# A four-head graph attention layer aggregated with its operands swapped: pairs of heads in column groups of TensorE

## The chip, the cores and the metric

The kernel runs on one core of one Trainium2 chip. The metric is device time in microseconds of one execution. Engines are named as in the profile: PE is TensorE's matmul side, PEld its weight loads, DVE VectorE, ACT ScalarE, POOL GpSimd, SP SyncE. A matmul holds one operand in the array (the weights, up to 128 columns) and streams the other past it (the moving operand, up to 512 columns); the result lands in PSUM with one partition for each weight column.

## The reference

Four graph attention layers with pre-layernorm and residuals work on x of shape (32, 512, 256) in float32, with one 512 x 512 adjacency. The change concerns the third one, with four heads of 64 features:

```python
Wh = (h @ W).reshape(h.shape[0], h.shape[1], N_H, D_F)
s_src = jnp.einsum('bnhd,hd->bnh', Wh, a_src)
s_dst = jnp.einsum('bnhd,hd->bnh', Wh, a_dst)
e = s_src[:, :, None, :] + s_dst[:, None, :, :]
e = jnp.where(e > 0, e, NEG_SLOPE * e)
e = jnp.where(mask, e, -jnp.inf)
alpha = jax.nn.softmax(e, axis=2)
h_out = jnp.einsum('bijh,bjhd->bihd', alpha, Wh)
...
x = x + jax.nn.elu(h_out)
```

The other three layers have one head of 256 features (the last one a small network with two attentions inside). Their kernels share the helpers shown below.

## The kernel before

A batch is 512 nodes by 256 features: `NT` = 4 tiles of 128 nodes, `KF` = 2 tiles of 128 features, `NH` = 4 heads of `D` = 64 features, `CH` = 67 columns for a head.

The softmax is factored. With a query's factor taken out, the weight of key j for query i is the larger of a row value of i and a column value of j, times the mask; a key's own factor is folded into its features. So a head's weights are four DVE instructions (`weights`, line 353), one for each tile j of 128 keys: 128 keys on partitions, 512 queries along the free dimension. The row values must stand on all partitions. For head 0 that is done by four transposes on PE into a bank of PSUM. For heads 1 to 3 it goes through memory: `rows_out` (line 362) transposes the 16 columns of values, copies them to `row`, writes them to memory, and `spread` (line 372) reads each head's row back onto 128 partitions, into one of two buffers. Both transfers are issued by SP, in order.

Aggregation of a head (lines 491 to 499): for each tile t of 128 queries, four matmuls over the key tiles j hold a 128 x 128 block of the head's weights in the array and stream 65 columns of `v`: 64 features and, as the 65th, the key's factor, whose sum is the denominator. All four t's lie in one PSUM bank. DVE then takes the reciprocal of the four denominators (`reciprocal`, line 385) and multiplies the features by it, out of PSUM into `ya`. After each second head, ACT makes exp and relu of the pair's 128 features for all nodes and DVE adds the ELU to x (`add_elu`).

The order of all work is written by a planner at build time. `NS` = 4 streams each take every fourth batch. A stream is a generator; what it emits between two `yield`s stands in the engines' queues as one block. It yields the planned time of its next block, and the main loop always takes the stream with the smallest one. `after_us(n)` is the planned time of the block's start plus `STRETCH` = 2 times the TensorE cycles that the block has counted (`spent`, at 2400 cycles a microsecond) plus `SLOW` = 1.5 times n. The helper `matmul` (line 64) counts four cycles for each moving column and at least 128 columns, `transpose` (line 68) counts 256 cycles. Each stream has two banks of PSUM (`bank`) and borrows those of streams that have not begun or have ended. The weights of all streams share four buffers (tag `w`).

In layer 2 a stream makes head 0's weights and the 4.5 us of `after_us(3)` later head 1's, and from then on a head's weights are begun one head ahead of their aggregation: `begin(h + 1)`, then a wait for the planned time of head h (4.8 us after its begin at the least), then 16 matmuls.

Of the kernel before, what the change touches and what calls it, by code (L numbers as in the profile page):

```python
# [19 lines left out]
FP = mybir.dt.float32  # L20
# [3 lines left out]
AF = mybir.ActivationFunctionType  # L24
OP = mybir.AluOpType
AX = mybir.AxisListType

EPS = 1.0e-5
P = 128
# [6 lines left out]
def fast(ctx, tc, flag, x, adj, w0, a0, w1, a1, w2, a2, mlp1_w, mlp1_b, mlp2_w, mlp2_b,  # L36
         w_fc, a_fc, w_hand, a_hand, out):
    nc = tc.nc
    B, N, F = x.shape
    NT = N // P  # L40
# [3 lines left out]
    NH = a2.shape[0]  # L44
    D = F // NH
# [6 lines left out]
    work = ctx.enter_context(tc.tile_pool(name="work", bufs=2))  # L52
# [5 lines left out]
    spent = [0.0]  # L58

    def after_us(us):  # L60

        return begun[0] + STRETCH * spent[0] / CYCLES + SLOW * us

    def matmul(p, w, x, **flags):
        spent[0] += 4 * max(x.shape[-1], P)
        nc.tensor.matmul(p, w, x, **flags)  # L66

    def transpose(p, x, i, tied=False):
        spent[0] += 2 * P
        instruction = nc.tensor.transpose(p, x, i)  # L70
        if tied:
            tc.keep_in_program_order(instruction)
# [4 lines left out]
    def bank():  # L77

        own = [turn[0], *(i for i in range(NS) if i not in active and i != turn[0])]
        banks[0] += 1  # L80
        return psum.tile([P, N], FP, tag=f"b{own[banks[0] % len(own)]}", name="b", bufs=8 // NS)
# [3 lines left out]
    ident = const.tile([P, P], FP, name="ident")  # L85
# [78 lines left out]
    for h in range(NH):  # L164
        t, r = divmod(h * D, P)
# [91 lines left out]
    def small(shape, name):  # L257
        return work.tile([P] + shape, FP, tag=name, name=name, bufs=2 * NS)

    def new_xn():  # L260
        return work.tile([P, NT, F], FP, tag="xn", name="xn", bufs=3)

    def norm(xt, xn, rs, t0, late):


        st = small([2, 6], "st")
        mv = small([2, 2], "mv")
        for i in range(2):
            nc.vector.bn_stats(st[:, i, :], xt[:, t0 + i, :])  # L269
            nc.vector.bn_aggr(mv[:, i, :], st[:, i, :])  # L270
        rp = rs[:, t0:t0 + 2]
        nc.scalar.activation(rp, mv[:, :, 1], AF.Ln, bias=eps)
        nc.scalar.activation(rp, rp, AF.Exp, scale=-0.5)
        for i in range(2):
            if late:
                nc.vector.tensor_scalar(
                    xn[:, t0 + i, :], xt[:, t0 + i, :], mv[:, i, 0:1], None, op0=OP.subtract
                )
            else:
                nc.vector.tensor_scalar(  # L280
                    xn[:, t0 + i, :], xt[:, t0 + i, :], mv[:, i, 0:1], rp[:, i:i + 1], op0=OP.subtract, op1=OP.mult
                )
# [9 lines left out]
    def turned(xn, when):  # L292

        hT = work.tile([P, KF, N], FP, tag="hT", name="hT", bufs=3)
        turn_pair(xn, hT, 0)
        yield when
        turn_pair(xn, hT, 2)
        yield after_us(0.6)
        return hT
# [3 lines left out]
    def note(e):  # L303

        c = next(noted)
        nc.vector.tensor_reduce(seen[:, c:c + 1], e, AX.XY, OP.max)
# [36 lines left out]
    def weights(r_col, t_col, masked=True, r=None):  # L343

        landed = r is not None
        if not landed:
            r = bank()
            for t in range(NT):
                transpose(r[:, t * P:(t + 1) * P], r_col(t).to_broadcast([P, P]), ident)
        wt = work.tile([P, NT, N], FP, tag="w", name="w", bufs=4)  # L350
        for j in range(NT):
            if masked:
                w = nc.vector.scalar_tensor_tensor(  # L353
                    wt[:, j, :], r, t_col(j), maskT[:, j, :], op0=OP.max, op1=OP.mult
                )
                if landed and j == 0:
                    tc.keep_in_program_order(w)
            else:
                nc.vector.tensor_scalar(wt[:, j, :], r, t_col(j), None, op0=OP.max)
        return wt  # L360

    def rows_out(cols, n):

        p = bank()
        transpose(p[:NT * n, :P], cols, ident)
        row = work.tile([P, P], FP, tag="row", name="row", bufs=1)[:NT * n, :]
        nc.scalar.copy(row, p[:NT * n, :P])
        row_d = dram.tile([n, N], FP, tag="row", name="row", bufs=4)
        nc.sync.dma_start(row_d.rearrange("n (t p) -> t n p", p=P), row)
        return row_d  # L370

    def spread(row):

        r = work.tile([P, N], FP, tag="spread", name="spread", bufs=2)
        nc.sync.dma_start(r, row.partition_broadcast(P))
        return r

    def pair(tag="y"):
        return work.tile([P, 2, F], FP, tag=tag, name=tag, bufs=3)

    def aggregate(p, wt, t, rhs):
        for j in range(NT):
            matmul(p, wt[:, j, t * P:(t + 1) * P], rhs(j), start=(j == 0), stop=(j == NT - 1))

    def reciprocal(den):
        r = small([1], "rden") if len(den.shape) == 2 else small([NH, 1], "rden4")
        nc.vector.reciprocal(r, den)  # L387
        return r

# [7 lines left out]
    def averages(v, wt, t):  # L397
        p = bank()
        aggregate(p[:, :F + 1], wt, t, lambda j: v[:, j, :F + 1])
        return p[:, :F], reciprocal(p[:, F:F + 1])  # L400


    def add_elu(xr, r, q):

        nc.vector.scalar_tensor_tensor(r, q, 1.0, r, op0=OP.min, op1=OP.add)  # L405
        nc.vector.scalar_tensor_tensor(xr, r, -1.0, xr, op0=OP.add, op1=OP.add)  # L406
# [45 lines left out]
    def layer2(xt, xn, rs, when):  # L452
        hT = yield from turned(xn, when)
        v = work.tile([P, NT, NH, CH], FP, tag="v", name="v2", bufs=4)
        for t in range(NT):
            ps = bank()
            for k in range(KF):
                matmul(
                    ps[:, :NH * CH], hT[:, k, t * P:(t + 1) * P], W2[:, k, :, :], start=(k == 0), stop=(k == KF - 1)
                )  # L460
            pv = ps[:, :NH * CH].rearrange("p (h c) -> p h c", c=CH)
            nc.scalar.activation(v[:, t, :, D:], pv[:, :, D:], AF.Exp, scale=rs[:, t:t + 1])
            nc.vector.scalar_tensor_tensor(  # L463
                v[:, t, :, :D], pv[:, :, :D], rs[:, t:t + 1], v[:, t, :, D:D + 1].to_broadcast([P, NH, D]),
                op0=OP.mult, op1=OP.mult,
            )
            yield after_us(0 if t + 1 < NT else 1)
        ya = work.tile([P, NT, F], FP, tag="y4", name="y4", bufs=1)
        wts = []

        def begin(h):
            wts.append(
                weights(
                    lambda t: v[:, t, h, D + 2:D + 3], lambda j: v[:, j, h, D + 1:D + 2], r=far[h]
                )
            )
            return after_us(3.2)

        row_d = rows_out(v[:, :, :, D + 2], NH)
        far = [spread(row_d[h, :]) if h else None for h in range(NH)]
        when = begin(0)
        note(v.rearrange("p t h c -> p (t h) c")[:, :, D:])
        yield after_us(3)
        for h in range(NH):
            last = when
            if h + 1 < NH:
                when = begin(h + 1)
            yield last  # L490
            wt = wts[h]
            p = bank()
            for t in range(NT):
                aggregate(p[:, t * (D + 1):(t + 1) * (D + 1)], wt, t, lambda j: v[:, j, h, :D + 1])
            pv = p[:, :NT * (D + 1)].rearrange("p (t c) -> p t c", c=D + 1)
            r = reciprocal(pv[:, :, D:])
            nc.vector.tensor_tensor(
                ya[:, :, h * D:(h + 1) * D], pv[:, :, :D], r.to_broadcast([P, NT, D]), op=OP.mult
            )
            if h % 2:  # L500
                c = slice((h - 1) * D, (h + 1) * D)
                y = ya[:, :, c]
                q = pair("q").rearrange("p a (b f) -> p (a b) f", f=2 * D)
                nc.scalar.activation(q, y, AF.Exp)  # L504
                nc.scalar.activation(y, y, AF.Relu)  # L505
                add_elu(xt[:, :, c], y, q)
            yield after_us(0)
        xn, rs = new_xn(), small([NT], "rs")
        for t0 in range(0, NT, 2):
            norm(xt, xn, rs, t0, False)  # L510
        yield after_us(7)
        return xn, rs, after_us(2)
# [257 lines left out]
    while ready:  # L770
        i = min(ready, key=ready.get)
# [23 lines left out]
    p = bank()  # L795
# [437 lines left out]
```

## Time and profile before

| what | value |
|---|---|
| median of 3 runs | 2935.77 us |
| lowest and highest run | 2931.55, 2940.25 us |
| span of the profiled execution, first to last instruction | 2929.6 us |
| instructions | 43083 |
| DMA moved in the span | 270.89 MB, mean 92 GB/s |
| mean granted TensorE clock | 0.996 |

The profiled execution's own time is known only as its span. It lies 6.2 us below the median of the runs.

In a group of instructions, a row gives line, engine, operation, output and inputs by the program's names, shape and count, then busy time in us and mean length of one in ns, then the engine's idle time just before them and what ended most of it. A shape such as 128\*128 128x65 is a matmul with 128 rows by 128 columns of weights and 65 moving columns. Line 66 and line 70 are the helpers `matmul` and `transpose`. In a timeline a row is start, length, engine, line, operation and count of a run of alike instructions.

### The profile page before, as it was taken

Reading aid. Unit: us, or ns where it says so; the run is one execution under the profiler, and the core shown is the slowest. Engines: PE = TensorE matmul, PEld = TensorE weight load, DVE = VectorE, ACT = ScalarE, POOL = GpSimd, SP = SyncE. Lnnn points to the kernel's source line nnn. Section 1 sums busy time; section 2 is a strip of 40 time slices with the busy share of each in tenths; the row PEclk is TensorE's granted clock in tenths of the full one; section 3 lists DMA queues with packets and bytes.
Section 4 is the critical chain, followed back from the end, with each engine's and each line's share of the span. In section 5 each row is a group of like instructions: output and inputs, shape, how many; then the busy total and the mean of one; then the engine's idle time right before and its main releaser. Section 6 shows DMA issues by size and latency. Waiting matters only on the chain.

```text
span 2929.6 us, 43083 instructions
## 1 busy us (share of the span) xinstructions
PE 2858.9 (98%) x15177; PEld 2329.5 (80%) x15177; DVE 2219.9 (76%) x5676; ACT 1536.8 (52%) x3922; POOL 502.3 (17%) x515
## 2 busy tenths in 40 slices
PE   8999999999999999999999999999999999999998
PEld 6777887877888877888877888788887788877876
DVE  4677877778778778778778777787787787777764
ACT  4444455555555555555554556545555555555444
POOL 0011112112122111122021121111221111211220
PEclk9999999999999999999999999999999999999999
DMA  3033223233223333233332233222332322323230
GB/s 94 19 102 102 80 88 116 91 98 95 88 94 106 93 100 98 84 102 96 100 102 80 89 115 93 91 97 91 94 116 80 102 93 88 104 93 96 90 107 30
DMA packets 193182, 270.89 MB, mean 92 GB/s; under 512 B 17024, under 2 KB 156094, under 8 KB 192960
## 3 DMA queue, kind: packets, MB, share of 16 engines
q1 hardware_dynamic: 163200, 169.76, 18.5%
q0 software_dynamic: 29760, 98.30, 10.4%
q8 instruction: 123, 2.02, 0.3%
q14 instruction: 99, 0.81, 0.1%
HBM read 152.62 MB, written 115.39 MB: 91 GB/s over the span
## 4 chain that ended last, share of the span: by engine, by line
PE 82%; DVE 10%; ACT 4%; DMA 3%; issue 1%; SPq 0%; POOL 0%; DVEq 0%; POOLq 0%; ACTq 0%
PE b L66 75%; PE b L70 7%; DVE st L269 2%; DMA g<-table,at 2%; DVE sums L641 1%; DVE xn L280 1%; DVE x L406 1%; DVE y L405 1%; ACT v L325 1%; DVE sums L632 1%; ACT y L505 1%; ACT q L504 1%; DVE w L353 1%; ACT hT L290 1%; DVE tot L646 0%
## 5 line engine op out<-in xcount | busy, mean ns | idle before, releaser
L66 PE MATMUL b<-v,w 128*128 128x65 f32 (+1 forms) x7232 | 1218.0, 321 | 10.6 <-DVE w L353 10.5
L66 PEld LDWEIGHTS b<-v,w 128*128 128x128 f32 x7232 | 1050.0, 191 | 168.7 <-issue 56.1
L66 PE MATMUL b<-WFC,oT 128*128 128x256 f32 (+1 forms) x2048 | 495.2, 380 | 0.0
L66 PEld LDWEIGHTS b<-WFC,oT 128*128 128x128 f32 x2048 | 374.5, 189 | 49.3
L66 PE MATMUL b<-W,hT 128*128 128x259 f32 (+1 forms) x1536 | 388.8, 391 | 22.8 <-DVE v L463 14.1
L353 DVE SCALAR_TENSOR_TENSOR w<-b,v,maskT 128x512 f32<-128x512 f32 x512 | 369.4, 744 | 5.1 <-PE b L70 4.1
L607 POOL DMA_INDIRECT order<-v,at x248 | 277.0, 1117 | 490.7 <-DVE oT L730 152.3
L66 PEld LDWEIGHTS b<-W,hT 128*128 128x128 f32 x1536 | 285.3, 192 | 75.3 <-DVE v L463 17.1
L715 POOL TENSOR_TENSOR x<-x,y 128x512 f32<-128x512 f32 x62 | 87.8, 1416 | 1063.7 <-ACT y L713 950.0
L353 DVE SCALAR_TENSOR_TENSOR w<-spread,v,maskT 128x512 f32<-128x512 f32 x384 | 269.5, 742 | 0.0
L66 PE MATMUL b<-hT,WM 128*128 128x512 f32 x512 | 250.0, 599 | 0.7 <-ACT hT L290 0.7
L66 PE MATMUL b<-oT,WM 128*128 128x512 f32 x512 | 231.2, 594 | 0.0
L655 POOL DMA_INDIRECT g<-table,at x124 | 120.9, 975 | 642.8 <-ACT y L675 292.0
L387 DVE RECIPROCAL rden<-b 128x1 f32<-128x1 f32 (+1 forms) x516 | 77.3, 162 | 184.8 <-PE b L66 183.0
L529 ACT ACTIVATE v<-b,ends 128x256 f32<-128x256 f32 x256 | 118.8, 467 | 177.2 <-PE b L66 172.9
L269 DVE BATCH_NORM_STATS2 st<-x 128x6 f32<-128x256 f32 x512 | 193.3, 409 | 6.4 <-DMA x<-in_x_dram 4.1
L412 DVE TENSOR_TENSOR y<-q,y 128x512 f32<-128x512 f32 (+1 forms) x194 | 132.9, 685 | 82.9 <-ACT q L411 45.0
L339 ACT ACTIVATE oT<-b,bias 128x512 f32<-128x512 f32 x128 | 87.7, 686 | 182.7 <-PE b L66 182.0
L290 ACT ACTIVATE hT<-b 128x512 f32<-128x512 f32 x256 | 146.5, 592 | 70.3 <-PE b L70 70.2
L66 PEld LDWEIGHTS b<-oT,WM 128*128 128x128 f32 x512 | 97.5, 191 | 95.7 <-issue 92.4
L70 PE MATMUL b<-ident,xn 128*128 128x128 f32 x1024 | 147.4, 275 | 6.7 <-DVE xn L280 4.0
L70 PEld LDWEIGHTS b<-ident,xn 128*128 128x128 f32 x1024 | 123.7, 143 | 31.9 <-DVE xn L280 5.2
(143 smaller groups left out, 3748.1 us busy)
## 6 DMA issues: line engine op xcount, KB each, us to landing
table<-sums SPq DMA_DIRECT2D x62, 1032.0 KB
sums<-order SPq DMA_DIRECT2D x62, 516.0 KB
spread<-row SPq DMA_DIRECT2D x96, 256.0 KB
x<-in_x_dram SPq DMA_DIRECT2D x32, 512.0 KB
out_dram<-x SPq DMA_DIRECT2D x62, 256.0 KB
sums<-order SPq DMA_DIRECT2D x62, 129.0 KB
order<-v,at POOLq DMA_INDIRECT x248
g<-table,at POOLq DMA_INDIRECT x124
```

Of the source, the lines that this page charges most:

```text
L66: nc.tensor.matmul(p, w, x, **flags)
L70: instruction = nc.tensor.transpose(p, x, i)
L269: nc.vector.bn_stats(st[:, i, :], xt[:, t0 + i, :])
L290: nc.scalar.activation(hT[:, :, t0 * P:(t0 + 2) * P], p.rearrange("p (k n) -> p k n", k=KF), AF.Relu)
L339: nc.scalar.activation(o[:, f, :], p, AF.Relu, bias=bias[:, f:f + 1])
L353: w = nc.vector.scalar_tensor_tensor(wt[:, j, :], r, t_col(j), maskT[:, j, :], op0=OP.max, op1=OP.mult)
L387: nc.vector.reciprocal(r, den)
L412: nc.vector.tensor_tensor(r, q, r, op=OP.add)
L529: nc.scalar.activation(halves[c][:, t, :F], ps[:, :F], AF.Copy, scale=ends[:, t, 0:1])
L607: nc.gpsimd.indirect_dma_start(out=orders[c], out_offset=bass.IndirectOffsetOnAxis(ap=at[:, 0, t:t + 1], axis=0), in_=halves[c][:, t, :], ...
L655: nc.gpsimd.indirect_dma_start(out=g, out_offset=None, in_=table, in_offset=bass.IndirectOffsetOnAxis(ap=at[:, 1, t:t + 1], axis=0),)
L715: (nc.gpsimd if n == 2 else nc.vector).tensor_tensor(xr, xr, y, op=OP.add)
```

## The change

The operands of layer 2's aggregation trade places, and heads are taken in pairs. The features of a head become the weights in the array, 64 columns of them, and the 512 queries of a key tile's softmax weights are the moving operand. The two heads of a pair are put into the two halves of the array's columns by `tile_position`, in a loop over key tiles with the heads inside. The denominators have matmuls of their own: the key's factor is repeated over 32 weight columns, and four groups of 32 columns take two heads by two halves of the key tiles. Results stand transposed (features, or sums, on partitions; queries along the free dimension). ACT copies both from PSUM to SBUF (`staged`), four transposes each bring them back (`turned_back`), DVE adds the two halves of the sums, takes reciprocals for both heads at once and multiplies. The exp, relu and residual of a pair are as before.

The blocks move too. Head 1's weights are begun in the block after head 0's with `after_us(0)`, the heads of the second pair both after the first pair's matmuls, and a pair is aggregated at the earliest 9 us (`after_us(6)`) after the second of its heads is begun. The transposes back stand in a block of their own, after the next pair's begins.

```diff
@@ -64,6 +64,10 @@
     def matmul(p, w, x, **flags):
         spent[0] += 4 * max(x.shape[-1], P)
         nc.tensor.matmul(p, w, x, **flags)
+
+    def beside(p, w, x, c, **flags):
+        spent[0] += 4 * x.shape[-1] * w.shape[-1] // P
+        nc.tensor.matmul(p, w, x, tile_position=(0, c), **flags)
 
     def transpose(p, x, i, tied=False):
         spent[0] += 2 * P
@@ -383,7 +387,7 @@
             matmul(p, wt[:, j, t * P:(t + 1) * P], rhs(j), start=(j == 0), stop=(j == NT - 1))
 
     def reciprocal(den):
-        r = small([1], "rden") if len(den.shape) == 2 else small([NH, 1], "rden4")
+        r = small([1], "rden")
         nc.vector.reciprocal(r, den)
         return r
 
@@ -465,7 +469,6 @@
                 op0=OP.mult, op1=OP.mult,
             )
             yield after_us(0 if t + 1 < NT else 1)
-        ya = work.tile([P, NT, F], FP, tag="y4", name="y4", bufs=1)
         wts = []
 
         def begin(h):
@@ -474,36 +477,68 @@
                     lambda t: v[:, t, h, D + 2:D + 3], lambda j: v[:, j, h, D + 1:D + 2], r=far[h]
                 )
             )
-            return after_us(3.2)
-
-
+
+        def staged(p):
+            s = work.tile([P, N], FP, tag="y4", name="y4", bufs=2)
+            nc.scalar.copy(s, p)
+            return s
+
+        def turned_back(s):
+            p = bank()
+            for t in range(NT):
+                transpose(p[:, t * P:(t + 1) * P], s[:, t * P:(t + 1) * P], ident)
+            return p
 
         row_d = rows_out(v[:, :, :, D + 2], NH)
         far = [spread(row_d[h, :]) if h else None for h in range(NH)]
-        when = begin(0)
+        begin(0)
         note(v.rearrange("p t h c -> p (t h) c")[:, :, D:])
-        yield after_us(3)
-        for h in range(NH):
-            last = when
-            if h + 1 < NH:
-                when = begin(h + 1)
-            yield last
-            wt = wts[h]
-            p = bank()
-            for t in range(NT):
-                aggregate(p[:, t * (D + 1):(t + 1) * (D + 1)], wt, t, lambda j: v[:, j, h, :D + 1])
-            pv = p[:, :NT * (D + 1)].rearrange("p (t c) -> p t c", c=D + 1)
-            r = reciprocal(pv[:, :, D:])
+        yield after_us(0)
+        begin(1)
+        when = after_us(6)
+        half = NT // 2
+        for g in range(0, NH, 2):
+            yield when
+            fp, sp = bank(), bank()
+            for j in range(half):
+                for i in range(4):
+                    e = i // 2, i % 2 * half + j
+                    beside(
+                        sp[i * 32:(i + 1) * 32, :], v[:, e[1], g + e[0], D:D + 1].to_broadcast([P, 32]),
+                        wts[g + e[0]][:, e[1], :], i * 32, start=(j == 0), stop=(j == half - 1),
+                    )
+            s = staged(sp)
+            for j in range(NT):
+                for i in range(2):
+                    beside(
+                        fp[i * D:(i + 1) * D, :], v[:, j, g + i, :D], wts[g + i][:, j, :], i * D,
+                        start=(j == 0), stop=(j == NT - 1),
+                    )
+            f = staged(fp)
+            yield after_us(1.5)
+            if g + 2 < NH:
+                begin(g + 2)
+                yield after_us(0)
+                begin(g + 3)
+                when = after_us(6)
+                yield after_us(1.5)
+            p = turned_back(s)
+            r = small([2 * NT], "rden8")
+            nc.vector.tensor_reduce(
+                r, p.rearrange("p (e s k) -> p e s k", s=2, k=32)[:, :, :, 0], AX.X, OP.add
+            )
+            nc.vector.reciprocal(r, r)
+            p = turned_back(f)
+            y, q = pair(), pair("q")
+            y = y.rearrange("p a (b f) -> p (a b) f", f=2 * D)
+            q = q.rearrange("p a (b f) -> p (a b) f", f=2 * D)
             nc.vector.tensor_tensor(
-                ya[:, :, h * D:(h + 1) * D], pv[:, :, :D], r.to_broadcast([P, NT, D]), op=OP.mult
-            )
-            if h % 2:
-                c = slice((h - 1) * D, (h + 1) * D)
-                y = ya[:, :, c]
-                q = pair("q").rearrange("p a (b f) -> p (a b) f", f=2 * D)
-                nc.scalar.activation(q, y, AF.Exp)
-                nc.scalar.activation(y, y, AF.Relu)
-                add_elu(xt[:, :, c], y, q)
+                y.rearrange("p t (h d) -> p (t h) d", d=D), p.rearrange("p (e d) -> p e d", d=D),
+                r.unsqueeze(2).to_broadcast([P, 2 * NT, D]), op=OP.mult,
+            )
+            nc.scalar.activation(q, y, AF.Exp)
+            nc.scalar.activation(y, y, AF.Relu)
+            add_elu(xt[:, :, g * D:(g + 2) * D], y, q)
             yield after_us(0)
         xn, rs = new_xn(), small([NT], "rs")
         for t0 in range(0, NT, 2):
```

## The prediction

> **What bounds the kernel now.** I read four views, in this order: the page's busy times and its chain, the groups with shapes kept apart, the matmul part of the timeline around one head of layer 2, and the vector and queue parts of the same stretch.
>
> ```profile
> PE 2858.9 (98%) x15177; PEld 2329.5 (80%) x15177; DVE 2219.9 (76%) x5676; ACT 1536.8 (52%) x3922; POOL 502.3 (17%) x515
> PEclk9999999999999999999999999999999999999999
> PE 82%; DVE 10%; ACT 4%; DMA 3%; issue 1%; SPq 0%; POOL 0%; DVEq 0%; POOLq 0%; ACTq 0%
> ```
>
> TensorE is busy for 98% of the span at the full granted clock (0.996 by the clock view), and it carries 82% of the chain that ended last. The other engines have room: DVE idles for 24%, about 22 us in each of the 32 batches (a batch is 2929.6 / 32 = 91.6 us). So a microsecond of matmul added or removed is first taken as a microsecond of span, and work of DVE or ACT counts only where TensorE has to wait for it.
>
> ```profile
> L66 PE MATMUL b<-v,w 128*128 128x65 f32 x4096 | 476.2, 273 | 1.0 <-DVE w L353 1.0
> L66 PE MATMUL b<-hT,WM 128*128 128x512 f32 x512 | 250.0, 599 | 0.7 <-ACT hT L290 0.7
> L70 PEld LDWEIGHTS b<-ident,v 128*16 128x16 f32 x32 | 3.0, 93 | 0.5
> L387 DVE RECIPROCAL rden<-b 128x4 f32<-128x4 f32 x128 | 22.7, 177 | 83.5 <-PE b L66 83.4
> L497 DVE TENSOR_TENSOR y<-b,rden 128x256 f32<-128x256 f32 x128 | 53.3, 416 | 1.1
> L353 DVE SCALAR_TENSOR_TENSOR w<-spread,v,maskT 128x512 f32<-128x512 f32 x384 | 269.5, 742 | 0.0
> L581 ACT COPY tj<-b 128x512 f32<-128x512 f32 x31 | 17.8, 576 | 1.7 <-PE b L70 1.7
> ```
>
> The first row is the work that the change replaces. The kernel asks for 32 batches x 4 heads x 16 = 2048 of these matmuls, and the row counts 4096: a float32 matmul is two passes, one right after the other, each with its own weight load. The means (273, 599 ns) are lengths of pipelined records that overlap; the cost of a pass is the distance from one start to the next, which the timeline gives (start, length, engine, line, operation):
>
> ```profile
> 1514.76 1.88 PE L66 MATMUL b<-hT,WM 128*128 128x512 f32 x4
> 1516.48 3.63 PE L66 MATMUL b<-v,w 128*128 128x257 f32 x16
> ...
> 1544.38 0.60 PE L70 MATMUL b<-ident,y 128*128 128x128 f32 x4
> 1544.81 0.71 PE L70 MATMUL b<-ident,v 128*16 128x128 f32 x5
> ...
> 1551.00 3.68 PE L66 MATMUL b<-v,w 128*128 128x65 f32 x32
> 1554.52 0.61 PE L70 MATMUL b<-ident,y 128*128 128x128 f32 x4
> ```
>
> A pass over 512 columns costs (1516.48 - 1514.76) / 4 = 0.43 us, a transpose of 128 columns, one pass, 0.43 / 4 = 0.108 us, and a pass over 65 columns (1554.52 - 1551.00) / 32 = 0.110 us. By its columns the last should cost 0.43 x 65 / 512 = 0.055; it costs as much as 128, because each pass loads 128 columns of weights first. That waste is what the change is aimed at.
>
> **The change part by part, for one pair of heads (64 pairs in all).**
>
> Removed: 2 heads x 32 passes x 0.110 = 7.04 us of TensorE.
>
> Added, sums: 8 matmuls of 32 weight columns over 512 moving columns, 16 passes of 0.43. Added, features: 8 matmuls of 64 weight columns over 512, another 16 passes. One after another they would take 32 x 0.43 = 13.76 us; the whole change rests on several running at once in different column groups. The trace of before has no instruction that uses part of the columns beside another, so I bound it. Upper end: one pass at a time, 13.76 us. Lower end: four at a time in the sums (4 x 0.43) and two in the features (8 x 0.43), 5.16 us. What I take lies between, and comes from the order of the passes. The loop issues group 0, then 1, 2, 3, but each matmul is two adjacent passes on the same group, and in this trace passes start strictly in the order of issue, each no earlier than the columns of its predecessor on those array columns are through. If that stays so, the second pass of group 0 waits 0.43 us for the first, and the first pass of group 1 stands behind it. Then second pass and next first pass run together, never more: two in flight, whether the groups are two or four. Sixteen passes then end after 9 x 0.43 = 3.87 us, for the sums and for the features alike: 7.74 us.
>
> Added, turning back: 8 transposes x 0.108 = 0.86 us, so 8.60 us in all. Going from full array to 32-column groups, to 64-column groups and back is three switches a pair. No row shows one; below, zero (the 128*16 transpose stands among full ones at the usual spacing, 0.55 us for five); above, a full run-out of the pipe, 0.272 - 0.108 = 0.16 us each, 0.49 a pair. I take the middle, 0.25. Sum: 8.85 - 7.04 = +1.81 us a pair, x 64 = +116 us.
>
> The Trainium skill ("TensorEngine Tiling (Array Packing)", Key Properties) says that tiles run in parallel but that a change of tiling mode drains the engine, which speaks against three switches for 7 us of work; no run here shows one yet. Its page "TensorE: Matmul & The Clock Gate" (Part 3) gives 2.38 times for three column groups and says that matmuls stay in program order; by an estimate from that efficiency, 6.9 / 3.2 + 6.9 / 1.6 + 0.9 = 7.4 us, some 20 us slower over the kernel, if the two passes did not stand in each other's way.
>
> Other engines. DVE loses two reciprocals (0.177) and two multiplications (0.416), 1.19 us, and gains one small reduction (nearest row, a reduction of 12 elements, 0.156), one reciprocal (0.177) and one 512-wide multiplication out of PSUM (nearest row 0.68): 1.01. ACT gains two copies of 0.576, 74 us over the kernel, 52% to 55% busy. I cost both at nothing: the sums' copy runs beside the features' matmuls, the features' copy beside other streams, since a planned 2.25 us beyond the pair's own matmuls lie before the transposes that need it. Uncovered, the second copy would cost 64 x 0.58 = 37 us; behind it on ACT stand other streams' evacuations, for which TensorE has two banks a stream.
>
> A wait that the change adds: the weights of head 1 now follow those of head 0 at once; the planned 3 x 1.5 = 4.5 us between them are gone. They read a row that travels out to memory and back.
>
> ```profile
> 1546.19 0.68 SPq L369 DMA_DIRECT2D row<-row  x1
> 1549.54 0.82 SPq L375 DMA_DIRECT2D spread<-row  x2
> ```
> ```profile
> 1546.25 2.72 DVE L353 SCALAR_TENSOR_TENSOR w<-b,v,maskT 128x512 f32<-128x512 f32 x4
> ...
> 1555.89 1.41 DVE L353 SCALAR_TENSOR_TENSOR w<-spread,v,maskT 128x512 f32<-128x512 f32 x2
> ```
>
> Over the 32 batches the broadcast lands 4.9 to 7.3 us after the row's copy (by its semaphore) and is first used at 9.7 to 10.4 in nearly all; 4.5 us earlier is 5.2 to 5.9, so DVE, with every stream's vector work queued behind, waits up to 2 us a batch, at most 64 us. Below nothing I see no gain in it. With TensorE loaded by 3.6 us more per batch and DVE idle for 22, I take zero and keep 64 for the range. On SP the last broadcast is held until head 1's weights are made (1550.42 to 1558.65 here); that now comes earlier, which costs nothing.
>
> The profiled span is 2929.6, the median of the runs 2935.77, 6.2 above. 2929.6 + 116 + 6.2 = 3052 us. This case alone spans 3036 (no switch cost) to 3131 (full run-out, 2 us of DVE a batch).
>
> **The rivals.**
>
> *Full overlap, the other side.* Each column group goes on by itself and four passes run at once: 5.16 + 0.86 = 6.02 us a pair, -65 us over the kernel. For it: the work is truly in different array columns. Against: the order of passes above. Less up to 0.49 for switches and up to 32 us of the DVE wait, which no longer hides: 2871 to 2934, middle 2905. The point from which it decides: 13.76 us of passes must fit into 7.04 - 0.86 - 0.25 = 5.93, a mean of 2.3 in flight. Below that the change loses.
>
> *Two in flight, weight loads in the open.* A load cannot go ahead of a waiting pass, so each change of group shows one: 14 a pair at 0.093 (16 columns) to 0.19 (128): about 0.13, +1.8 us a pair on the 1.81: +3.6 x 64 = +231, 3167 us. For it: in the trace a load starts with the pass before it and never earlier.
>
> *No overlap.* 13.76 + 0.86 + 0.25 - 7.04 = +7.83 a pair, 3437 us. For it: nothing before shows two matmuls at once.
>
> *Full overlap eaten by the wait for the broadcast*, slightly slower: 2945 to 2960.
>
> **How the numbers follow.** Two in flight 0.36, with open loads 0.17, full overlap 0.30, none 0.14, eaten 0.03. About 0.3%, 9 us, is what a measurement of this kernel can tell from no change. Of the full overlap 0.22 is faster by that, 0.05 within it and 0.03 slower; everything else is slower: 0.73. The range leaves out no overlap and the very best of full overlap: 2890 to 3210; the likeliest case's own is 3030 to 3130.
>
> **What would show it.** Right: in the profile after, the 512-column rows on 32 and 64 columns start in pairs 0.43 us apart, a block of 16 passes takes 3.9 us, TensorE's busy time rises by about 100 us and DVE's idle time too. Four starts together, blocks of 1.7 and 3.4 us, make the rival right; starts 0.43 apart one by one, no overlap. An idle TensorE that waits for weights of head 1 would make the cost of the moved step wrong, and a granted clock below 0.99 all of it.

## The result, and the profile after

The changed kernel takes 3246.68 us (median of 4 runs, 3237.79 to 3261.80) against 2936.86 us before: 1.106 times as long, 95% interval 1.103 to 1.110, or 310 us slower. The forecast of slower was right. Its 3052 us missed by 195 us, and its range ended at 3210.

First the page of the changed kernel (the engines' busy times, the granted clock by slices, two of the costliest groups), then its groups with shapes kept apart.

```profile
PE 3025.8 (93%) x13641; PEld 2034.0 (63%) x13641; DVE 2233.7 (69%) x5612; ACT 1631.9 (50%) x4050; POOL 486.2 (15%) x515
PEclk9999999999999999999999999999999999999999
...
L357 DVE SCALAR_TENSOR_TENSOR w<-spread,v,maskT 128x512 f32<-128x512 f32 x384 | 264.9, 745 | 76.7 <-DMA spread<-row 76.7
...
L483 ACT COPY y<-b 128x512 f32<-128x512 f32 x128 | 74.9, 586 | 273.2 <-PE b L70 272.9
```
```profile
L70 PE MATMUL b<-w,v 128*64 128x512 f32 x1024 | 278.4, 605 | 0.0
...
L70 PE MATMUL b<-w,v 128*32 128x512 f32 x1024 | 210.3, 622 | 23.9 <-DVE w L357 23.9
```

TensorE was busy for 98% of the span and is now busy for 93%: it runs out of work. The new matmuls are busy for about as long (489 us in the two rows) as the old row was (476 us), and no longer than the 495 us that the forecast had for them. Line 70 is now `beside`, line 74 `transpose`, line 66 still `matmul`, line 357 the weights on DVE, line 483 the copies.

The timeline shows how they run, and why the forecast of their time was wrong.

```profile
1535.53 0.60 PE L66 MATMUL b<-v,w 128*128 128x257 f32 x2
1536.06 2.17 PE L70 MATMUL b<-w,v 128*32 128x512 f32 x16
1538.16 3.70 PE L66 MATMUL b<-oT,WM 128*128 128x512 f32 x8
1541.79 3.65 PE L70 MATMUL b<-w,v 128*64 128x512 f32 x16
1545.37 2.00 PE L66 MATMUL b<-v,w 128*128 128x257 f32 x8
...
1610.87 1.05 PE L70 MATMUL b<-w,v 128*32 128x512 f32 x4
1613.93 1.84 PE L70 MATMUL b<-w,v 128*32 128x512 f32 x4 [2.02 <-DVE w L357]
```

Sixteen passes of 512 columns in four groups take 2.1 us from start to next start, sixteen in two groups 3.58, where one after another they would take 6.9. Four run at once, and two: full overlap. But the sums and the features of one pair do not stand together. The framework that builds the program orders each engine's queue by its own estimate of what is ready; here it put eight passes of another stream (`oT,WM`) between them. In the built program the array changes between its three column modes 387 times, where 64 pairs need 192. At 1610.87 four passes of a block have run, and the rest waits 2.02 us for weights. In the same stretch DVE shows why those come late:

```profile
1613.13 1.41 DVE L357 SCALAR_TENSOR_TENSOR w<-spread,v,maskT 128x512 f32<-128x512 f32 x2 [2.38 <-DMA spread<-row]
```

The waits of the changed kernel (who waited for what, us in total, times, longest) show which engine stands still for what.

```profile
ACT y L483 <- PE b L70: 272.9, 112, 9.6
...
DVE sums L662 <- DMA sums<-order: 160.7, 57, 11.4
...
DVE w L357 <- DMA spread<-row: 76.7, 32, 4.4
```

And the same view of the kernel before:

```profile
DVE sums L627 <- DMA sums<-order: 28.8, 28, 3.2
```

DVE now stands still for two transfers, 76.7 us for the broadcast rows, which it never waited for before, and 160.7 us for the sorted rows of layer 3, for 28.8. What stands behind such an instruction in DVE's queue comes later, and what ACT and TensorE wait for comes later with it, as at 1613.13; how much of the whole loss goes this way no view says.

TensorE's time can be split. *Streaming* is worked out from the starts of all matmul records, with 0.8375 ns for a moving column and a pass, 0.108 us for a transpose, 0.110 us for a 65-column pass, and time that passes share counted once. It is 2779 us before and 2820 after, so the work itself adds 41 us. A mode switch shows as 0.094 us of idle array (median over the 387), and the first full pass after one takes 0.106 us longer; with about 0.05 on the first pass in groups (1541.79 to the next on its group at 1542.27, 0.48 for 0.43) that is some 65 us. The rest of the 310 is idle time (TensorE idles for 221 us of its span, 71 before) and clock.

The Trainium skill ("TensorEngine Tiling (Array Packing)", Key Properties) holds on both counts here: tiles ran in parallel, and a change of mode cost 0.09 to 0.2 us each. Its page "TensorE: Matmul & The Clock Gate" (Part 1) says that an idle window of about 3.4 us halves the clock until a busy one has passed. The clock record has half-rate stretches, most of them of 3.4 and 6.8 us, 116 us of the span after and 25 before. But the window ahead of them was not idle throughout: ahead of 27 of the 29 stretches after, TensorE was busy for 10 to 44% of the 3.4 us. TensorE worked for 103 and 20 us of the half-rate time, so by an estimate it lost 52 and 10 us there: the loss feeds on itself, by some 42 us.

### The profile page after: what moved, and what is told of

Its sections match the earlier page's. It is cut to its first block, busy times and chain, and to the rows that moved or that the text cites. A ratio compares the mean times of both kernels' runs of the same rounds, so it can differ in the third digit from the quotient of the medians.

```text
span 3246.5 us, 40133 instructions
## 1 busy us (share of the span) xinstructions
PE 3025.8 (93%) x13641; PEld 2034.0 (63%) x13641; DVE 2233.7 (69%) x5612; ACT 1631.9 (50%) x4050; POOL 486.2 (15%) x515
## 5 line engine op out<-in xcount | busy, mean ns | idle before, releaser
L66 PE MATMUL b<-v,w 128*128 128x257 f32 (+1 forms) x3136 | 783.7, 390 | 40.5 <-ACT y L444 20.6
L66 PEld LDWEIGHTS b<-v,w 128*128 128x128 f32 x3136 | 578.9, 192 | 219.3 <-DVE w L357 60.5
L70 PE MATMUL b<-w,v 128*64 128x512 f32 (+1 forms) x2048 | 483.6, 614 | 23.9 <-DVE w L357 23.9
L66 PE MATMUL b<-W,hT 128*128 128x259 f32 (+1 forms) x1536 | 402.4, 397 | 24.9 <-ACT v L329 21.4
L357 DVE SCALAR_TENSOR_TENSOR w<-b,v,maskT 128x512 f32<-128x512 f32 x512 | 357.7, 744 | 12.8 <-PE b L74 10.2
L642 POOL DMA_INDIRECT order<-v,at x248 | 258.1, 1041 | 468.2 <-ACT q L415 110.5
L357 DVE SCALAR_TENSOR_TENSOR w<-spread,v,maskT 128x512 f32<-128x512 f32 x384 | 264.9, 745 | 76.7 <-DMA spread<-row 76.7
L70 PEld LDWEIGHTS b<-w,v 128*64 128x64 f32 (+1 forms) x2048 | 110.6, 123 | 308.6 <-issue 212.2
L483 ACT COPY y<-b 128x512 f32<-128x512 f32 x128 | 74.9, 586 | 273.2 <-PE b L70 272.9
L74 PE MATMUL b<-ident,xn 128*128 128x128 f32 x1024 | 164.5, 281 | 42.8 <-DVE xn L280 33.8
L294 ACT ACTIVATE hT<-b 128x512 f32<-128x512 f32 x256 | 149.2, 597 | 74.3 <-PE b L74 73.4
L74 PE MATMUL b<-ident,y 128*128 128x128 f32 x1024 | 152.4, 277 | 22.9 <-DVE y L416 22.9
```

The source lines that it names most:

```text
L70: nc.tensor.matmul(p, w, x, tile_position=(0, c), **flags)
L294: nc.scalar.activation(hT[:, :, t0 * P:(t0 + 2) * P], p.rearrange("p (k n) -> p k n", k=KF), AF.Relu)
L357: w = nc.vector.scalar_tensor_tensor(wt[:, j, :], r, t_col(j), maskT[:, j, :], op0=OP.max, op1=OP.mult)
L483: nc.scalar.copy(s, p)
L642: nc.gpsimd.indirect_dma_start(out=orders[c], out_offset=bass.IndirectOffsetOnAxis(ap=at[:, 0, t:t + 1], axis=0), in_=halves[c][:, t, :], ...
```

## The experiments

In the table, *plan* is the length that the kernel's own planner gives layer 2 of a batch, in planned us (52.8 before). It stood in no forecast; what it is worth is the question of e5 to e7.

| kernel | us | plan | streaming | switches |
|---|---|---|---|---|
| before | 2936.9 | 52.8 | 2779 | 0 |
| after | 3246.7 | 69.8 | 2820 | 387 |
| e1 old matmuls, new blocks | 3291.6 | 74.9 | 2779 | 0 |
| e2 gap restored | 3139.5 | 74.3 | 2771 | 282 |
| e3 after, TensorE in source order | 3644.2 | 69.8 | 2741 | 192 |
| e4 before, TensorE in source order | 3351.3 | 52.8 | 2780 | 0 |
| e5 before, longer plan | 3075.3 | 74.3 | 2779 | 0 |
| e6 short waits | 3158.4 | 61.4 | 2833 | 362 |
| e7 half counted | 3076.1 | 51.2 | 2831 | 437 |
| e8 half counted, fenced | 3136.5 | 51.2 | 2755 | 192 |
| e9 gap restored, fenced | 3203.7 | 74.3 | 2728 | 192 |
| e10 before, gap removed | 3025.2 | 48.3 | 2779 | 0 |
| e11 ready blocks | 3000.9 | 56.5 | 2762 | 278 |
| e12 old matmuls, ready blocks | 3101.4 | 58.2 | 2781 | 0 |

**e1: the old matmuls in the new blocks.** Is it the work or its place?

```diff
             yield when
-            fp, sp = bank(), bank()
-            ... (sums, copy, features, copy)
+            ps = []
+            for h in (g, g + 1):
+                p = bank()
+                for t in range(NT):
+                    aggregate(p[:, t * (D + 1):(t + 1) * (D + 1)], wts[h], t, lambda j: v[:, j, h, :D + 1])
+                ps.append(p)
             yield after_us(1.5)
```

> The old 65-column matmuls, reciprocal and multiplication, in the blocks of the change: both heads of a pair begun one after the other, aggregated together at the earliest 9 us later, read out in a later block. No column groups, no copies, no transposes back. Theory W (the loss comes from waits that the new blocks bring in: VectorE sat 77 us for the broadcast row and 161 us for the sorted sums, against 0 and 29 before): this is slower than before by 130 to 250 us. Theory P (the loss is TensorE's own new work: 41 us more of streaming and some 65 us of switches between column modes, and what follows from it): within 30 us of before.

It took 3291.56 us, 1.121 times before (1.119 to 1.124): without a single column group it is slower than the change. Theory W had the sign and 130 to 250 us; it is 355. The page has TensorE's clock down with it:

```profile
PE 3056.0 (93%) x15177; PEld 2462.2 (75%) x15177; DVE 2231.5 (68%) x5676; ACT 1565.4 (48%) x3922; POOL 485.4 (15%) x515
...
PEclk9998899988999989989999899998899988999899
```

The loss is in how the blocks are laid, not in what they compute. Streaming is that of before to the microsecond; the rest is waiting, and 410 us at half rate.

**e2: the old gap between heads 0 and 1.**

```diff
-        yield after_us(0)
+        yield after_us(3)
         begin(1)
```

> The changed kernel with the old 4.5 planned us between head 0's and head 1's weights put back, nothing else. Theory W in its narrow form (the wait for the broadcast row, 77 us of VectorE, is handed on to TensorE): 60 to 120 us faster than the changed kernel, so about 3130 to 3190. Theory P: within 25 us of the changed kernel, save for what fewer mode switches give (282 in the built order for 387, at 0.1 to 0.2 us each 10 to 20 us).

3139.47 us, 107 us faster than the change. The wait for the rows shrinks from 76.7 to 23.5 us, while that for the sorted rows grows:

```profile
DVE sums L662 <- DMA sums<-order: 257.1, 62, 14.3
...
DVE w L357 <- DMA spread<-row: 23.5, 12, 3.5
```

A moved step whose cost was put at nothing is worth a third of the loss. Streaming falls by 49 us and the switches by 105 with it, so not all of the 107 us is the wait itself; e10 has the step without them. The other 203 us stay, although streaming is now 8 us below before.

**e3 and e4: TensorE in the order of the source**, to put each pair's matmuls together; e4 does the same to the kernel before.

```diff
-        nc.tensor.matmul(p, w, x, **flags)
+        tc.keep_in_program_order(nc.tensor.matmul(p, w, x, **flags))
```

> The changed kernel with every TensorE instruction kept in the order in which the source emits it, so that the column-group matmuls of a pair stand together: 192 mode switches in the built order for 387, no full-array matmul inside a group of four. Theory P: sums and features stream in 110 and 220 us for 178 and 251, and switches fall by half, so 100 to 140 us faster than the changed kernel, about 3110 to 3150. Theory W: the waits stay or grow, since TensorE can no longer go on with something else; 30 us faster to 100 us slower than the changed kernel.

> Control for the run before it: the kernel before with every TensorE instruction kept in the order of the source. Both theories: slower than before by 0 to 60 us, since the order of the build was chosen over that of the source; what it loses is to be taken from what the run before it shows.

3644.15 and 3351.27 us: the tie costs 397 us on the change and 414 on the kernel before. Both missed their expectations by far; as a test of the switches the pair is spoilt, and it says only that the framework's freedom to fill gaps is worth 400 us here. The change is 293 us behind in source order too.

**e5: the kernel before with a longer plan.** By then the planned lengths had been set beside the times: the change makes layer 2 of the plan 17 us longer, e2 21.5. A stream works on one batch at a time, so with four streams the kernel needs at least a quarter of a batch's chain for each batch; before, a round of four batches took 2936.9 / 8 = 367 us, of which 2779 / 8 = 347 us are streaming. How much of the 367 us one batch's chain fills, no view says; the idea under test is that it leaves little.

```diff
+        yield after_us(14.3)
         xn, rs = new_xn(), small([NT], "rs")
```

> The kernel before, with nothing changed but one planned wait of 21.5 us put into layer 2 of each batch, so that the plan gives a batch's layer 2 74.3 us for 52.8, as it does in the run with the gap restored (the plan's end goes from 2578 to 2750 us). No operation is added or moved within the layer. Theory C (a stream works on one batch at a time, so the length of a batch's chain in the plan sets the period, and TensorE just runs dry): the measured time follows the plan, 2750 x 1.139 = 3131 us, within 40. Theory W (the loss is made by particular waits: the broadcast row, the sorted sums, the copies): within 30 us of before, since none of these is touched. Theory P: the same as before.

3075.26 us, 1.048 times before (1.045 to 1.050). Adding a planned wait and nothing else costs 143 us. That rules out the two theories that had no change; theory C gave 3131 us within 40, so the cost is 73% of its figure and just short of its range. It also brings out the wait for the sorted rows in a kernel that touches neither rows nor sort (28.8 us before):

```profile
DVE sums L628 <- DMA sums<-order: 111.0, 54, 6.6
```

So at least a part of that wait in the change follows from the plan, and not from anything done to the rows or the sort. Of the 203 us that e2 left, 143 are what the same planned length costs the kernel before; the 60 that remain are near the price of e2's 282 switches, about 45 us by the figures above. That these costs simply add up is argued, not shown: e5 is one wait at one place, and no run separates a longer plan from another order in which the four streams meet.

**e6 and e7: shorter plans for the new matmuls.** Both restore the gap, wait 4.8 planned us ahead of a pair for 9, drop the 2.25 planned us behind it, and begin head 2 ahead of the first pair; e7 also counts the column-group matmuls at half.

```diff
-                when = after_us(6)
+                when = after_us(3.2)
...
-        spent[0] += 4 * x.shape[-1] * w.shape[-1] // P
+        spent[0] += 2 * x.shape[-1] * w.shape[-1] // P
```

> The new matmuls, copies and transposes, with a shorter plan: the old 4.5 planned us between heads 0 and 1, 4.8 planned us instead of 9 ahead of a pair, no 2.25 us behind a pair, head 2 begun ahead of the first pair's matmuls. The plan gives layer 2 61.4 us (end of the plan 2646). Theory C: 2646 x 1.14 = 3016 us, within 40. Theory P: 3140 or slower, since TensorE does the same work and has more mode switches in the built order (362 for 282).

> As the run before it, and the column-group matmuls are counted in the plan at half their cycles (a planned microsecond for one of TensorE instead of two). The plan gives layer 2 51.2 us, its end is at 2564. Theory C: TensorE's own work bounds it again, 2771 us of streaming and some 50 of switches against 2779, so 2900 to 2975, the same as before within 1.3%. Theory P: above 3050.

3158.39 and 3076.08 us. Theory C missed both times: a plan shorter by 13 us than e2's gained nothing, and the plan of before did not give the time of before. The length of the plan alone does not set the time. The groups of e7, and below them those of e2, show what a shorter plan did here:

```profile
L70 PE MATMUL b<-w,v 128*64 128x512 f32 x1024 | 280.7, 604 | 0.0
...
L70 PE MATMUL b<-w,v 128*32 128x512 f32 x1024 | 218.3, 601 | 1.4 <-DVE w L357 1.4
```
```profile
L70 PE MATMUL b<-w,v 128*64 128x512 f32 x1024 | 262.1, 601 | 0.0
...
L70 PE MATMUL b<-w,v 128*32 128x512 f32 x1024 | 154.1, 599 | 1.9 <-DVE w L357 1.9
```

499 us for what e2 does in 416: when a pair's turn comes before its weights are made, the framework breaks its block up with other work, groups run alone, and each break is two switches. Against before, e7 has 52 us more streaming and 437 switches, some 65 to 75 us; these make up most of its 144.

**e8 and e9: the blocks kept together by fences** (the first matmul of a pair behind what other streams have emitted, the rest in a chain, the next 24 instructions behind the block), on e7 and on e2.

```diff
+        if head:
+            for name in last.values():
+                behind(ins, name)
+        else:
+            behind(ins, fence[0])
+        fence[0], fence[1] = ins.ins.name, 24
```

> As the half-counted run, and the 16 column-group matmuls of a pair kept together: the first is queued behind what the other streams have already emitted on TensorE, each next one behind the last, and the next 24 TensorE instructions of any stream behind the block. 192 mode switches in the built order for 437. Theory S (what is left of the loss at 3076 is broken-up blocks: 52 us more streaming than before and some 65 us of switches): streaming falls to about 2721 us and switches to about 30, 2950 to 2990 us. Theory F (a fence makes TensorE wait for what it is fenced behind, as the order of the source did): 3080 or slower.

> As the run with the gap restored (longer plan, 9 planned us ahead of a pair, so that the weights are ready when the block comes), with the same fences: 192 mode switches for 282. Streaming was 2771 us there and 42 us of switches. Theory S: 50 us less streaming and 15 us less switching, but TensorE already waits for the plan, so 20 to 60 us faster than that run: 3080 to 3120 us. Theory F: slower than that run's 3139.

3136.45 and 3203.68 us: each about 60 us slower than without fences, although streaming fell to 2755 and 2728 us and switches to 192. Theory F holds. In e9, sixteen passes in four groups stream in 116 / 64 = 1.8 us, 3.8 times one by one: the overlap is as good as it gets, and TensorE pays for it by idling: 278 us of the span for 191 in e2. Its longest waits are for vector work of other blocks (a transpose, line 95 here, waits for layer 3's `y`), more than for weights (23.7 us):

```profile
PE b L95 <- DVE y L438: 84.3, 34, 5.5
```

**e10: the moved step alone, on the kernel before.**

```diff
-        yield after_us(3)
+        yield after_us(0)
         for h in range(NH):
```

> The kernel before with one step of the change alone: head 1's weights are begun right after head 0's, without the 4.5 planned us between them. The plan gets shorter by that (layer 2 48.3 us for 52.8, end at 2542). If the wait for the broadcast row is what made the restored gap worth 107 us: VectorE waits 60 to 90 us for it here too and the kernel is 30 to 120 us slower in spite of the shorter plan. If that run gained by something else: the same as before or faster, within 20 us.

3025.16 us, 1.031 times before (1.030 to 1.033): 92 us slower with a plan that is 4.5 us shorter. DVE's wait is there:

```profile
DVE w L353 <- DMA spread<-row: 52.6, 25, 3.0
```

TensorE idles for 116 us of the span (71 before) and is at half rate for 108 (25 before), with the same streaming. One line of the change costs 92 us on one kernel and 107 on the other. It also shows that a shorter plan can be slower.

**e11 and e12: blocks that are ready, with both kinds of matmul.** e11 counts half as e7 does, restores the gap, has no planned wait behind a pair and waits 7.5 planned us ahead of it, long enough that the built order holds its blocks together better (278 switches); e12 has the old matmuls in the same blocks.

```diff
-        when = after_us(6)
+        when = after_us(5)
...
-            yield after_us(1.5)
+            yield after_us(0)
```

> The new matmuls with 7.5 planned us ahead of a pair (5 counted for 6 in the change and 3.2 in the half-counted run), the old gap between heads 0 and 1, no planned wait behind a pair, and the column-group matmuls at half their cycles in the plan. The plan gives layer 2 56.5 us; the built order has 278 mode switches, and its runs of column-group matmuls would stream in 367 us for 438 in the half-counted run. Weighed by what the runs so far showed: 3076 less 70 of streaming and 24 of switches, more 30 for the longer plan, 3010 us, within 40. If TensorE's waits grow by as much as its work shrinks, as with the fences: 3060 to 3100.

> The old 65-column matmuls, reciprocals and multiplications in the blocks and waits of the run before it, their cycles in the plan halved too, so that the plans are nearly alike (layer 2 58.2 us for 56.5, end 2621 for 2608). If the new matmuls are worth something where the blocks suit them: this is slower than 3001 by 20 to 80 us (17 us of streaming and what the longer plan costs, less some 42 us of switches that it does not have, more the longer time that its two heads hold TensorE). If what is left of the loss at 3001 is the new work's own: this is faster than 3001, near 2960.

3000.88 us, 1.022 times before (1.020 to 1.024), inside the 3010 within 40 that was expected; and 3101.42 us, 1.058 (1.055 to 1.061), 100 us behind e11, where 20 to 80 were expected. The groups of e11:

```profile
L70 PE MATMUL b<-w,v 128*64 128x512 f32 x1024 | 251.3, 599 | 0.0
L70 PE MATMUL b<-w,v 128*32 128x512 f32 x1024 | 153.6, 599 | 0.1
```

In like blocks the new matmuls are 100 us faster than the old ones, and in the blocks of the change 45 us (e1). In the blocks of pairs the operands' swap is a gain. The blocks themselves are the loss (with the old matmuls 165 us in e12 and 355 in e1), and no version here makes up for it. Heads one by one with the new matmuls were not tried.

## Why the prediction was wrong, point by point

TensorE's own sum came out near by luck: 116 us were forecast, and the figures above give 41 of streaming and 65 of switches, 106. The overlap was taken 66 us too dear, the switches 49 too cheap and the removed passes 8 too dear. What failed is the step from that sum to the time: the waits of the new blocks, put at nothing, make up most of the other 204 us (TensorE idles 150 us more, and the half-rate clock costs some 42).

- *What bounds the kernel.* TensorE at 98% was read rightly, the conclusion was not: "a microsecond of matmul added or removed is first taken as a microsecond of span". In e2 and e9 streaming is 8 and 51 us below before, and the kernels are 203 and 268 us slower; in e1 it is the same, and the kernel is 355 us slower. The profile showed a full TensorE and could not show how little it takes to let it run dry, since TensorE itself hardly waited yet (71 us idle).
- *Two in flight, from the order of passes.* This step failed, though it is not what made the forecast too short. That "the first pass of group 1 stands behind it" was wrong: at 1536.06 the first passes of three groups start within 13 ns, and each group's second pass 0.45 us later. Streaming of sums and features is 178 + 251 = 429 us, not 64 x 7.74 = 495. The trace does not tell whether groups have queues of their own or the two passes of a matmul are not issued side by side. A full-array trace could not show either; the rival of full overlap, held at 0.30, was right in its mechanism.
- *Switches.* 0 to 0.16 us each was the right size (0.09, and up to 0.2 on the way back), but three a pair was counted from the source. The framework's order made six: 387.
- *Removed work and transposes.* 7.04 us a pair were 451 us and are 443 by starts; the added transposes are 55 us, as forecast.
- *Copies and DVE's arithmetic at nothing.* The durations were right (copy 586 ns, multiplication 687 for 680, reduction 164 for 156). ACT sat 273 us for the matmuls ahead of its copies; what that costs was not separated.
- *The wait for the broadcast row, taken as zero with 64 us kept.* "With TensorE loaded ... and DVE idle for 22, I take zero" failed. Its length was a little over the bound (at most 64 us: 76.7 in 32 waits, longest 4.4). Its price was far above that: 107 us for the step in e2, and 92 alone in e10, where DVE waits only 52.6. In e10 TensorE idles for 45 us more and loses clock; that all streams' vector work stands behind the wait is the likely reason for so high a price.
- *The blocks' planned length.* Not in the sum at all, and probably the largest term: 143 us by e5 for 21.5 planned us, by proportion some 113 for the change's 17 (an estimate; no run has that length alone, and e6, e7 and e10 show that the time does not simply follow the length). The front of this document names `after_us(6)`, the 9 us that it makes, and the doubled count of cycles; adding these up along one batch gives 17 planned us on the 299 that the plan has for a round, 5.7%, before any trace.
- *Rivals.* "Full overlap" had the streaming right, the sign wrong. "Full overlap eaten by the wait for the broadcast", at 0.03 and 2945 to 2960, was the kind of thing that happened, with about a twentieth of the loss.

## What to carry to other kernels

When several streams hide each other's waits, a busy engine is only half of the bound: the other half is when each stream's next block is ready. Here a planned chain 7% longer (21.5 of 299 planned us, e5) cost 4.8% with no work added, and one block begun too early (e10) cost 3.1%. Before pricing instructions, add up the planned waits along one chain before and after, and look for every wait that is moved nearer to the transfer it depends on. A cheaper operation that needs more of its inputs at once (two heads for one) has to be charged for that readiness.

## What the runs showed that was not expected

Float32 matmuls in different column groups of the array overlap almost perfectly: in e9 sixteen passes of 512 columns took 1.8 us in four groups and 3.5 us in two, for 6.9 one after another, and their weight loads were hidden. An early turn breaks that up: the same passes were busy for 416 us in e2 and 499 in e7. In the changed kernel the granted clock went to half after windows of 3.4 us in which TensorE was still busy for up to 44%. Holding TensorE to the order of the source cost 400 us, on either kernel, although every pass was the same.
